# A graph network kernel on one core: row sums of the adjacency by ScalarE instead of TensorE products, adjacency loads behind x, and part of the rows of the first loop by ScalarE

## The chip, the core and the metric

The kernel runs on one core of a Trainium2 chip. A core has five engines with a queue each: TensorE (PE in the profile), VectorE (DVE), ScalarE (ACT), GpSimd (POOL) and SyncE (SP), and 16 DMA engines that all queues share. The metric is the device time of one execution in microseconds, lower is better.

## What is computed

The reference runs four graph layers on x of shape (8, 2048, 64), each followed by a residual and a layer norm. All use one 2048 x 2048 matrix adj of zeros and ones with a diagonal of ones. Only the first two layers matter here:

```python
# layer 0: attention over hyperedges (g), mixed with a mean over neighbours (industry)
deg = jnp.maximum(adj.sum(-1), 1.0)[:, None]
industry = jnp.einsum('nm,bmf->bnf', adj / deg, x @ W_ind)
pair = jnp.stack([industry, g], axis=2)
coefs2 = jax.nn.softmax(attn_scores(pair), axis=-1)
out = jnp.einsum('bnk,bnkf->bnf', coefs2, pair)
# layer 1: symmetric normalisation
A_td = A + jnp.eye(n)
dinv = jax.lax.rsqrt(jnp.sum(A_td, axis=1))
A_hat = dinv[:, None] * A_td * dinv[None, :]
X_p = jnp.einsum('bnd,kd->bnk', jnp.einsum('bmd,nm->bnd', X, A_hat), W)
```

Both need the row sums of adj (the degrees): layer 0 as a reciprocal, layer 1 as an inverse root.

## The kernel before

The eight batches are four pairs p (two batches of 64 features fill 128 partitions). The adjacency is held in SBUF transposed, as 16 row tiles t of 128 rows, each in two halves g of 1024 columns: 32 loads of 512 KB by `load_adj` on POOL's queue (line 214). A product of x with the adjacency is split in a high and a low part so that it keeps its accuracy: for each pair and each half g, 16 tiles x 2 parts x 2 column chunks = 64 passes of 128x512 (line 175, helper `mm`).

The stages that the change touches, in order of time:

1. *The loop over h* (lines 568 to 617). For each of 16 tiles t: products of x with W into `ph` (two buffers in PSUM), clipped scores `seen` (585) and `lr` (592) on VectorE, two small exponentials on ScalarE (590, 596), two VectorE products into the row store `st` (599), one into `ex` (603), and the product `pagg` (609). Each pair of tiles is stored to HBM from ScalarE's queue (607). Five halves of adjacency are issued ahead of the loop behind the loads of x tiles 1 and 3 (`after`, 458), and five more within it, after tiles 1, 3, 5, 7 and 9 (`paced`).
2. *The slot stage* (lines 743 to 780). 16 tiles of rows, gathered in an order by degree, have 12, 5, 5, 4, 4, 4, 3, 3, 3, 3, 2, 2, 2, 2, 2 and 1 slots: 57. A slot is three products into `pz` (three buffers), a VectorE product (765), an exponential `y` on ScalarE (767), two VectorE operations (769, and 774 or 772) and an addition to `acc` on POOL (775). Beside each slot the loop draws five passes from the generator `products` (`fill(5)`, 757) and three more per tile (`fill(3)`), and issues two adjacency loads on POOL until all are out.
3. *The mix stage* (lines 958 to 986): 16 steps (pair p, chunk c) that weigh the neighbour mean against g. Each step loads a chunk of `u0_hbm` and of `inv_hbm` (`mix_load`, 810) and draws four times 8 or 9 passes from `all_pairs`, which gives what is left of `products` and then the products of layer 1 for each pair. Layer 1 of pair p needs the mixed chunks of pair p, stored, loaded again and scaled by `dinv` (`l1_parts`, 888). What is left after the last step is drawn behind it (the tail).

`products` (line 318) gives the 8 x 64 passes of u = adj times x, and behind the first of them 64 passes with a matrix of ones: `degrees` (322) multiplies `ones_r` by every tile, so that the column sums of the transposed adjacency stand in `du`. `inverses` (335) turns them to columns by four transposes, makes `dinv` on POOL (343) and the reciprocal on VectorE (344, 345), and writes the latter spread over 128 partitions to `inv_hbm`.

The order of each engine's queue is fixed when the program is built. TensorE's follows the text (`keep_in_program_order`), POOL's in part, while ScalarE's and VectorE's are set by a scheduler, from buffers and its own times. Each queue is worked in order.

Of the kernel before, what the change touches and what calls it, by code (L numbers as in the profile page):

```python
# [56 lines left out]
def tile_gnn_fast(  # L57
# [3 lines left out]
    x_n: bass.AP,  # L61
    x_t: bass.AP,
    adj_t: bass.AP,
    h_nt: bass.AP,
    h_e2: bass.AP,
    first: bass.AP,
# [31 lines left out]
    def cols(c, n=C):  # L98
        return slice(c * n, (c + 1) * n)
# [74 lines left out]
    def mm(*args, **kw):  # L174
        tc.keep_in_program_order(nc.tensor.matmul(*args, **kw))  # L175
# [40 lines left out]
    def adj_c(t, c):  # L216

        return adj[t][c // 2][:, cols(c % 2)]
# [6 lines left out]
    ones_r = hy.tile([P, P], F32R, name="ones_r")  # L225
    nc.vector.tensor_copy(ones_r, ones)
# [4 lines left out]
    deg4 = hy.tile([P, C], F32, name="deg4")  # L231


    HROW = BF + 8 + E
# [69 lines left out]
            pending.pop(0)[1]()  # L304

    places = {}
    xc, part = {}, {}

    mixed, free = set(), set()
# [8 lines left out]
    def products():  # L318

        deg1 = hy.tile([P, NT], F32, name="deg1")  # L320

        def degrees(g):
            du = pph.tile([P, 2, C], F32, tag="ph", name=f"du{g}", bufs=2)
            for t in range(NT):
                for i in range(2):
                    mm(
                        du[:, i, :], lhsT=ones_r, rhs=adj_c(t, 2 * g + i), start=t == 0, stop=t == NT - 1
                    )
                    yield
            for i in range(2):  # L330
                c = 2 * g + i
                r = slice(c * P // NCH, (c + 1) * P // NCH)
                evacuate(deg4[r, :], du[r, i, :])

        def inverses():

            pdc = places["small"]([P, JT, P], "pdc")
            for j in range(JT):
                transpose(pdc[:, j, :], deg4[:, cols(j, P)])
            pdc = pdc.rearrange("p j (c r) -> p c j r", c=NCH)[:, :, :, 0]  # L340
            d1 = deg1.rearrange("p (c j) -> p c j", c=NCH)
            nc.vector.tensor_scalar(d1, pdc, 1.0, None, op0=ALU.add)
            nc.gpsimd.tensor_tensor(dinv, deg1, neg_half[:, :NT], ALU.pow)
            nc.vector.tensor_scalar(d1, pdc, 1.0, None, op0=ALU.max)
            nc.vector.reciprocal(deg1, deg1)
            for _ in range(8):
                yield
            for c in range(NCH):
                pt = places["small"]([P, C], "pinv")
                for j in range(JT):  # L350
                    k = c * JT + j
                    transpose(pt[:, cols(j, P)], deg1[:, k:k + 1].to_broadcast([P, P]))
                row = va.tile([P, C], F32, tag="ut", name="inv", bufs=2)
                nc.scalar.copy(row, pt)
                nc.sync.dma_start(inv_hbm[:, cols(c)], row)
                for _ in range(4):
                    yield

        for p in range(NP):
            for g in range(2):  # L360
                own = (2 * g, 2 * g + 1)
                ug = pph.tile([P, 2, C], F32, tag="ph", name="ug", bufs=2)
                u = {c: ug[:, c % 2, :] for c in own}
                turning = inverses() if p == 0 and g == 1 else iter(())
                for t in range(NT):
                    for i in range(2):
                        for c in own:
                            mm(
                                u[c], lhsT=part[t // JT][i][:, t % JT, :], rhs=adj_c(t, c),
                                start=t == 0 and i == 0, stop=t == NT - 1 and i == 1,  # L370
                            )
                            tick()
                            if t > 1:
                                next(turning, None)
                            yield
                    if p == NP - 1 and g == 1 and t % JT == JT - 1:
                        first_parts(t // JT, free)
                    if p + 1 < NP and t % JT == JT - 1:
                        c = t // JT
                        if g == 1:  # L380
                            parts(p + 1, c)
                        if g == 1 and c < 2 or g == 0 and c >= 2:
                            fetch(p + 1, (c + 2) % NCH)
                if p == NP - 1:

                    for t in range(g * NT // 2, (g + 1) * NT // 2):
                        onto_diagonal(t, nc.gpsimd, ALU.add)
                for c in own:
                    ut = va.tile([P, C], F32, tag="ut", name="ut", bufs=2)
                    nc.scalar.copy(ut, u[c])  # L390
                    nc.sync.dma_start(u0_hbm[p][:, cols(c)], ut)
                if p == 0 and g == 0:
                    yield from degrees(0)
                    yield from degrees(1)

    def fill(n):
        for _ in range(n):
# [13 lines left out]
    with tc.tile_pool(name="pa_ps", bufs=1, space=PSUM) as pps:  # L411
# [159 lines left out]
        for t in range(NT):  # L571
# [56 lines left out]
        for c in (2, 3):  # L628
            fetch(0, c)
            parts(0, c)  # L630
        for t in range(len(paced) + 5, NT):
            load_adj(t, 0)
        to_load = [(t, 1) for t in range(NT)]
        pa_scope.close()
# [79 lines left out]
    with ExitStack() as pb_scope:  # L714
# [33 lines left out]
        for k, t in enumerate(tiles):  # L748
            S, both, ohs, R, co = now
            acc = pl.tile([P, B, F], F32, tag="acc", name="acc", bufs=2)  # L750
            for s in range(S):
                pz = pps.tile([P, C], F32, tag="mm", name="pz", bufs=3)
                for i, (l, r) in enumerate(((ident_r, both[0]), (ident_r, both[1]), (ohs[s], tab2))):
                    mm(pz, lhsT=l, rhs=r, start=i == 0, stop=i == 2)
                if s == 0 and k + 1 < NT:
                    fill(3)
                    now = begin(tiles[k + 1])
                fill(5)
                for _ in range(2):
# [5 lines left out]
                nc.vector.tensor_tensor(z, z, R[:, s, :, None].to_broadcast([P, B, F]), ALU.mult)  # L765
                y = pl.tile([P, B, F], F32, tag="y", name="y", bufs=3)
                nc.scalar.activation(y, z, AF.Exp, bias=-1.0)
# [42 lines left out]
    def mix_load(i):  # L810
        if i < steps:
            p, c = divmod(i, NCH)
            uts[i] = mp0.tile([P, C], F32, tag="ut0", name="ut0", bufs=2)
            nc.sync.dma_start(uts[i], u0_hbm[p][:, cols(c)])
            invs[i] = mp0.tile([P, C], F32, tag="inv0", name="inv0", bufs=2)
            nc.sync.dma_start(invs[i], inv_hbm[:, cols(c)])

    def mix_ind(i):
# [135 lines left out]
            yield from layer1(p)  # L954


    remaining = filler
    filler = all_pairs()
    mix_load(0)
# [492 lines left out]
def tile_gnn_general(  # L1452
# [640 lines left out]
    "emb", "emb_t", "w_pool", "b_pool", "iv", "w31_t", "b31", "w32_t", "b32",  # L2093
)
FAST = (
    "x_n", "x_t", "adj_t", "h_nt", "h_e2", "first", "mixing", "w1_t", "emb", "emb_4", "w_pool", "b_pool",
    "iv", "w31_t", "b31", "w32_t", "w32", "b32",
)


# [88 lines left out]
```

## Time and profile before

| | |
|---|---|
| device time, median of 3 runs | 1979.12 us (1975.02 to 1979.89) |
| the profiled execution | 1976.23 us, of which the profile's span is 1974.4 us |
| mean granted TensorE clock in it | 0.98 |
| TensorE busy | 1870.6 us (95% of the span) |
| VectorE busy | 1001.6 us (51%) |
| ScalarE busy | 394.6 us (20%) |
| GpSimd busy | 530.7 us (27%) |
| moved by DMA | 143.10 MB, mean 72 GB/s |

The profile is one execution recorded by the hardware; the span is what it covers, a little less than the time of that execution. Busy shares are means over stages with different limits. Matmuls are pipelined, so that their recorded lengths overlap: what a pass costs is read from the distance of two starts. "Idle before" names how long an engine stood still before an instruction and who released it. What an edit is worth is read from the stage that it is in: which wait ends last there.

### The profile page before, as it was taken

What the parts mean: (1) busy time and instruction counts of PE and PEld (TensorE: products, weight loads), DVE (VectorE), ACT (ScalarE), POOL (GpSimd) and SP (SyncE); (2) the same over time, 40 slices, a digit from 0 to 9 for tenths busy, and PEclk for the clock granted to TensorE, in tenths of its full rate; (3) what the DMA queues carried; (4) which work ended last, traced back from release to release, by engine and by line L of the source; (5) the groups of instructions that cost most, each with busy time, mean ns of one, the idle gap of its engine ahead of it and who ended that gap; (6) DMA issues with size and microseconds to landing.
All of it is one profiled execution on the core that took longest, in us unless ns stands there. A gap on an engine that the chain in (4) does not pass through costs nothing.

```text
span 1974.4 us, 19582 instructions
## 1 busy us (share of the span) xinstructions
PE 1870.6 (95%) x7100; PEld 1214.4 (62%) x7100; DVE 1001.6 (51%) x1741; ACT 394.6 (20%) x771; POOL 530.7 (27%) x480
## 2 busy tenths in 40 slices
PE   6888899888799999999999999999999999999997
PEld 4666566555554444755565575556546787877875
DVE  7779555556432211347546736764786333343332
ACT  1455343333121121100000000000001222222211
POOL 3678654544254344301001100110001020100101
PEclk9999899899899999999999999999999999999998
DMA  9923334332400000301101110111101122121211
GB/s 310 314 88 106 125 123 145 125 115 71 155 17 27 0 27 22 119 30 49 64 35 43 55 50 27 48 62 35 43 32 34 38 55 52 46 56 48 54 27 24
DMA packets 94185, 143.10 MB, mean 72 GB/s; under 512 B 29232, under 2 KB 40112, under 8 KB 93696
## 3 DMA queue, kind: packets, MB, share of 16 engines
q1 hardware_dynamic: 83920, 105.39, 17.2%
q0 software_dynamic: 7760, 27.66, 4.2%
q10 hardware_dynamic: 2400, 8.72, 1.2%
q8 instruction: 58, 0.95, 0.2%
q14 instruction: 47, 0.39, 0.1%
HBM read 98.67 MB, written 43.06 MB: 72 GB/s over the span
## 4 chain that ended last, share of the span: by engine, by line
PE 76%; DVE 4%; DMA 4%; POOL 4%; issue 3%; ACT 1%; SPq 1%; POOLq 0%; DVEq 0%; ACTq 0%
PE u L175 32%; PE py L175 22%; PE ua L175 11%; PE ug L175 3%; PE pr L175 2%; POOL ln_r L154 2%; PE po L175 1%; PE pf L175 1%; PE pt L178 1%; PE s L175 1%; DMA x<-x_hbm 1%; POOL r L906 1%; DMA r<-in_x_n 1%; DMA x_hbm<-r 1%; PE pd L175 0%
## 5 line engine op out<-in xcount | busy, mean ns | idle before, releaser
L175 PE MATMUL py<-wp,xg 128*128 128x512 f32 x1024 | 475.2, 592 | 0.7 <-DMA xg<-u_hbm 0.7
L175 PEld LDWEIGHTS py<-wp,xg 128*128 128x128 f32 x1024 | 193.3, 189 | 161.4 <-issue 138.5
L1276 DVE TENSOR_TENSOR fcav<-py,emb_n 128x512 f32<-128x512 f32 x256 | 177.0, 691 | 134.9 <-PE py L175 129.1
L175 PE MATMUL ua<-pt,xn 128*128 128x512 f32 x512 | 230.2, 592 | 1.5 <-DVE pt L1058 1.5
L154 POOL TENSOR_TENSOR ln_r<-ln_e,neg_half 128x8 f32<-128x8 f32 x64 | 108.1, 1688 | 458.0 <-DVE ln_e L152 425.0
L1277 DVE TENSOR_REDUCE r<-fcav 128x32 f32<-128x512 f32 x256 | 175.6, 686 | 8.2
L175 PEld LDWEIGHTS ua<-pt,xn 128*128 128x128 f32 x512 | 96.9, 190 | 110.9 <-issue 104.0
L175 PE MATMUL u<-adj,v0h 128*128 128x512 f32 x384 | 148.7, 455 | 1.3 <-ACT h L1432 1.3
L175 PE MATMUL u<-adj,v0l 128*128 128x512 f32 x384 | 141.3, 436 | 0.0
L175 PE MATMUL u<-adj,v2l 128*128 128x512 f32 x384 | 139.9, 429 | 1.2 <-DVE v2l L171 1.2
L175 PE MATMUL u<-adj,v2h 128*128 128x512 f32 x384 | 141.0, 433 | 0.0
L175 PE MATMUL u<-adj,v1h 128*128 128x512 f32 x384 | 140.7, 433 | 0.0
L175 PE MATMUL u<-adj,v3l 128*128 128x512 f32 x384 | 138.7, 426 | 0.0
L175 PE MATMUL u<-adj,v1l 128*128 128x512 f32 x384 | 138.4, 427 | 0.0
L175 PE MATMUL u<-adj,v3h 128*128 128x512 f32 x384 | 138.3, 427 | 0.0
L1063 POOL TENSOR_TENSOR acc<-acc,pt 128x512 f32<-128x512 f32 x60 | 76.8, 1280 | 103.9 <-DVE pt L1058 103.2
L1058 DVE TENSOR_SCALAR pt<-pt 128x512 f32<-128x512 f32 x64 | 30.2, 472 | 146.5 <-ACT pt L1057 146.2
L1358 DVE SCALAR_TENSOR_TENSOR ar<-fcav,ar 128x512 f32<-128x512 f32 x64 | 45.4, 709 | 109.1 <-ACT ar L1357 109.1
L175 PEld LDWEIGHTS u<-adj,v0h 128*128 128x128 f32 x384 | 71.6, 191 | 37.3 <-issue 24.5
L175 PEld LDWEIGHTS u<-adj,v2l 128*128 128x128 f32 x384 | 72.4, 190 | 32.2 <-issue 16.4
L175 PEld LDWEIGHTS u<-adj,v1l 128*128 128x128 f32 x384 | 72.8, 190 | 29.2 <-issue 14.4
L175 PEld LDWEIGHTS u<-adj,v3l 128*128 128x128 f32 x384 | 72.0, 188 | 29.4 <-issue 14.9
(354 smaller groups left out, 2669.5 us busy)
## 6 DMA issues: line engine op xcount, KB each, us to landing
adj<-in_adj_t POOLq DMA_DIRECT2D x32, 512.0 KB, 7.5
fcav<-in_adj_t SPq DMA_DIRECT2D x64, 256.0 KB, 2.9
u_hbm<-ut SPq DMA_DIRECT2D x48, 256.0 KB, 2.9
xg<-u_hbm SPq DMA_DIRECT2D x96, 128.0 KB, 2.9
x_hbm<-r SPq DMA_DIRECT2D x28, 256.0 KB, 2.1
hs_hbm<-st ACTq DMA_DIRECT2D x8, 584.0 KB
xt<-in_x_t SPq DMA_DIRECT2D x16, 256.0 KB, 6.6
ut<-u_hbm SPq DMA_DIRECT2D x16, 256.0 KB, 3.1
```

Of the source, the lines that this page charges most:

```text
L154: nc.gpsimd.tensor_tensor(rstd, vare, neg_half[:, :groups], ALU.pow)
L175: tc.keep_in_program_order(nc.tensor.matmul(*args, **kw))
L178: tc.keep_in_program_order(nc.tensor.transpose(dst, src, ident))
L906: nc.gpsimd.tensor_tensor(r, r, x1, ALU.add)
L1058: nc.vector.tensor_scalar(pt, pt, 1.0, None, op0=ALU.max)
L1063: nc.gpsimd.tensor_tensor(accs[c], accs[c], pt, ALU.add)
L1276: nc.vector.tensor_tensor(pr, py, e_b, ALU.mult)
L1277: nc.vector.tensor_reduce(r[:, j, b, cols(k, OH)], pr, AX.X, ALU.add)
L1358: nc.vector.scalar_tensor_tensor(ar.bitcast(F32), seen_a, 1.0, ar.bitcast(F32), op0=ALU.mult, op1=ALU.not_equal, accum_out=left[:, t, k:k ...
```

## The change

The degrees no longer come from products. The adjacency is given a second time in its natural layout (`adj_n`), and 32 pieces of 128 rows by 1024 columns are loaded on SP's queue into two buffers; ScalarE sums each along its row (`accum_out`). The generator `inverses` with these sums starts at pass 90 of the products instead of behind them. The reciprocals get a buffer of their own (`degs`). The two buffers of the pieces are later those of the mix stage's chunks. In the loop over h, adjacency loads wait for the first eight x tiles; two instead of five are issued ahead of the loop, seven within it, seven behind it. Of the two products into `st` one stays on VectorE and the other becomes four activations. In the slot stage's first tile four passes are drawn beside each slot instead of five.

```diff
-    def degrees(g):
-            du = pph.tile([P, 2, C], F32, tag="ph", name=f"du{g}", bufs=2)
-            for t in range(NT):
-                for i in range(2):
-                    mm(
-                        du[:, i, :], lhsT=ones_r, rhs=adj_c(t, 2 * g + i), start=t == 0, stop=t == NT - 1
-                    )
...
+        def inverses():
+            halves = [(t, g) for t in range(NT) for g in range(2)]
+            loaded = []
+            def load():
+                if halves:
+                    t, g = halves.pop(0)
+                    piece = mp0.tile([P, 2, C], F32, tag="uti", name="piece", bufs=2)
+                    flat = piece.rearrange("p k c -> p (k c)")
+                    nc.sync.dma_start(flat, adj_n[t * P:(t + 1) * P, g * N // 2:(g + 1) * N // 2])
+                    loaded.append((flat, t, g))
+            load()
+            load()
+            while loaded:
+                for _ in range(6):
                     yield
+                flat, t, g = loaded.pop(0)
+                nc.scalar.activation(flat, flat, AF.Identity, accum_out=deg2[:, t, g:g + 1])
+                load()
+            nc.vector.tensor_tensor(degs, deg2[:, :, 0], deg2[:, :, 1], ALU.add)
+            nc.vector.tensor_scalar(deg1, degs, 1.0, None, op0=ALU.add)
             nc.gpsimd.tensor_tensor(dinv, deg1, neg_half[:, :NT], ALU.pow)
-            nc.vector.tensor_scalar(d1, pdc, 1.0, None, op0=ALU.max)
-            nc.vector.reciprocal(deg1, deg1)
+            nc.vector.tensor_scalar(degs, degs, 1.0, None, op0=ALU.max)
+            nc.vector.reciprocal(degs, degs)
...
-                            if t > 1:
-                                next(turning, None)
+                            passes += 1
+                            if passes == 90:
+                                turning.append(inverses())
+                            if turning:
+                                next(turning[0], None)
                             yield
...
-                if p == 0 and g == 0:
-                    yield from degrees(0)
-                    yield from degrees(1)
...
-        for t in range(5):
-            if t in (0, 2):
-                after(xt[1 + t][:, 0, 0:1])
+        after(xt[2 * XB - 1][:, 0, 0:1])
+        for t in range(2):
             load_adj(t, 0)
...
-        paced = {1: 5, 3: 6, 5: 7, 7: 8, 9: 9}
+        paced = {1: 2, 3: 3, 5: 4, 7: 5, 9: 6, 11: 7, 13: 8}
...
-            for k in range(2):
-                nc.vector.scalar_tensor_tensor(
-                    st[:, k * G * F:(k + 1) * G * F].rearrange("p (g f) -> p g f", f=F), hv[:, k, :, 0:F], 1.0,
-                    e_gn[:, k * G:(k + 1) * G, None].to_broadcast([P, G, F]), op0=ALU.add, op1=ALU.mult,
+            nc.vector.scalar_tensor_tensor(
+                st[:, 0:G * F].rearrange("p (g f) -> p g f", f=F), hv[:, 0, :, 0:F], 1.0,
+                e_gn[:, 0:G, None].to_broadcast([P, G, F]), op0=ALU.add, op1=ALU.mult,
+            )
+            for g in range(G):
+                b = G + g
+                nc.scalar.activation(
+                    st[:, b * F:(b + 1) * F], hv[:, 1, g, 0:F], AF.Identity, bias=e_gn[:, b:b + 1], scale=e_gn[:, b:b + 1]
                 )
...
-                fill(5)
+                fill(4 if k < 1 else 5)
...
-            uts[i] = mp0.tile([P, C], F32, tag="ut0", name="ut0", bufs=2)
+            both = mp0.tile([P, 2, C], F32, tag="uti", name="uti", bufs=2)
+            uts[i], invs[i] = both[:, 0, :], both[:, 1, :]
...
+    for _ in turning[0]:
+        pass
     remaining = filler
```

More of the change, by code (lines that the diff above doesn't have):

```diff
@@ L63, in tile_gnn_fast @@
     adj_t: bass.AP,
+    adj_n: bass.AP,
     h_nt: bass.AP,
@@ L223, in onto_diagonal @@
         eng.tensor_tensor(block, block.bitcast(F32), ident, op)
-    ones_r = hy.tile([P, P], F32R, name="ones_r")
-    nc.vector.tensor_copy(ones_r, ones)
     number = hy.tile([P, 12], F32, name="number")
@@ L229, in tile_gnn_fast @@
         nc.gpsimd.memset(number[:, i:i + 1], -1.0 - i)
-    deg4 = hy.tile([P, C], F32, name="deg4")
+    deg2 = hy.tile([P, NT, 2], F32, name="deg2")
     HROW = BF + 8 + E
@@ L306, in tile_gnn_fast @@
     places = {}
+    turning = []
     xc, part = {}, {}
@@ L320, in products @@
         deg1 = hy.tile([P, NT], F32, name="deg1")
-        def degrees(g):
-            du = pph.tile([P, 2, C], F32, tag="ph", name=f"du{g}", bufs=2)
-            for t in range(NT):
-                for i in range(2):
-                    mm(
-                        du[:, i, :], lhsT=ones_r, rhs=adj_c(t, 2 * g + i), start=t == 0, stop=t == NT - 1
-                    )
-                    yield
[L330 to L342, printed above, removed]
+        degs = hy.tile([P, NT], F32, name="degs")
+        def inverses():
[12 more added lines that the diff above has]
+                for _ in range(6):
+                    yield
+                flat, t, g = loaded.pop(0)
[3 more added lines that the diff above has]
+            nc.vector.tensor_scalar(deg1, degs, 1.0, None, op0=ALU.add)
             nc.gpsimd.tensor_tensor(dinv, deg1, neg_half[:, :NT], ALU.pow)
-            nc.vector.tensor_scalar(d1, pdc, 1.0, None, op0=ALU.max)
-            nc.vector.reciprocal(deg1, deg1)
+            nc.vector.tensor_scalar(degs, degs, 1.0, None, op0=ALU.max)
+            nc.vector.reciprocal(degs, degs)
             for _ in range(8):
@@ L351, in inverses @@
                     k = c * JT + j
-                    transpose(pt[:, cols(j, P)], deg1[:, k:k + 1].to_broadcast([P, P]))
+                    transpose(pt[:, cols(j, P)], degs[:, k:k + 1].to_broadcast([P, P]))
                 row = va.tile([P, C], F32, tag="ut", name="inv", bufs=2)
@@ L357, in inverses @@
                     yield
+        passes = 0
         for p in range(NP):
@@ L363, in products @@
                 u = {c: ug[:, c % 2, :] for c in own}
-                turning = inverses() if p == 0 and g == 1 else iter(())
                 for t in range(NT):
@@ L630, in tile_gnn_fast @@
             parts(0, c)
-        for t in range(len(paced) + 5, NT):
+        for t in range(len(paced) + 2, NT):
             load_adj(t, 0)
@@ L812, in mix_load @@
             p, c = divmod(i, NCH)
-            uts[i] = mp0.tile([P, C], F32, tag="ut0", name="ut0", bufs=2)
+            both = mp0.tile([P, 2, C], F32, tag="uti", name="uti", bufs=2)
+            uts[i], invs[i] = both[:, 0, :], both[:, 1, :]
             nc.sync.dma_start(uts[i], u0_hbm[p][:, cols(c)])
-            invs[i] = mp0.tile([P, C], F32, tag="inv0", name="inv0", bufs=2)
             nc.sync.dma_start(invs[i], inv_hbm[:, cols(c)])
@@ L2095 @@
 FAST = (
-    "x_n", "x_t", "adj_t", "h_nt", "h_e2", "first", "mixing", "w1_t", "emb", "emb_4", "w_pool", "b_pool",
-    "iv", "w31_t", "b31", "w32_t", "w32", "b32",
+    "x_n", "x_t", "adj_t", "adj_n", "h_nt", "h_e2", "first", "mixing", "w1_t", "emb", "emb_4", "w_pool",
+    "b_pool", "iv", "w31_t", "b31", "w32_t", "w32", "b32",
 )
@@ L2146 @@
         "x_t": xt,
+        "adj_n": a["adj"],
         "x_n": xn,
```

## The prediction

> **What bounds the kernel now.** I read the page's slices first, then busy time by stretches, then the DMA queues, the waits and the timeline of each stage that the change touches. Four slices of the page:
>
> ```profile
> PE   6888899888799999999999999999999999999997
> ACT  1455343333121121100000000000001222222211
> DMA  9923334332400000301101110111101122121211
> GB/s 310 314 88 106 125 123 145 125 115 71 155 17 27 0 27 22 119 30 49 64 35 43 55 50 27 48 62 35 43 32 34 38 55 52 46 56 48 54 27 24
> ```
>
> A slice is 49 us. From about 550 us on TensorE is 9 tenths busy in almost every slice and the change touches nothing there. It touches the first eleven slices: the loop over h (to 54 us), the slot stage (65 to 235), the mix stage (239 to 493) and its tail (to 556). In the first two slices the DMA engines are full. Stretches:
>
> ```profile
> 60.00:80.00 20.00, 18.56 (x80) 14.93 (x79) 14.33 (x39) 8.49 (x27) 15.56 (x21) 0.83 1.01 343
> 80.00:100.00 20.00, 16.73 (x69) 11.82 (x69) 14.26 (x23) 8.60 (x23) 15.34 (x19) 1.00 1.10 364
> 100.00:120.00 20.00, 17.98 (x79) 13.64 (x78) 19.74 (x34) 11.31 (x31) 14.99 (x12) 1.00 0.15 53
> ...
> 160.00:180.00 20.00, 18.52 (x87) 14.67 (x86) 19.62 (x32) 10.13 (x29) 17.26 (x14) 1.00 0.25 81
> ```
>
> The columns are PE, PE load, DVE, ACT, POOL, granted clock, DMA share, GB/s. To 100 us the transfers are saturated (share 1.0 to 1.1); from 100 us VectorE is (19.6 to 19.7 of 20), and TensorE has slack. A product that leaves this stage therefore buys little in it. What fills the DMA engines is this, from the DMA view of 70 to 80 us:
>
> ```profile
> q0 software_dynamic: 1118, 4.10, 112.9%
> issues: line engine op xcount, KB each, median us to landing
> adj<-in_adj_t POOLq DMA_DIRECT2D x7, 512.0 KB, 7.5
> ```
>
> 4.10 MB in 10 us is 410 GB/s, all of it adjacency, and a half row block takes 7.5 us to land. In the slot stage's first tile ScalarE's timeline shows how the exponentials (y) hang on VectorE:
>
> ```profile
> 75.71 0.60 ACT L767 ACTIVATE y<-pz 128x512 f32<-128x512 f32 x1 [1.36 <-DVE pz L765]
> 77.68 0.60 ACT L767 ACTIVATE y<-pz 128x512 f32<-128x512 f32 x1 [1.36 <-DVE pz L765]
> 79.70 0.60 ACT L767 ACTIVATE y<-pz 128x512 f32<-128x512 f32 x1 [1.42 <-DVE pz L765]
> ```
>
> One slot each 1.97 us, ScalarE idle two thirds of it: room in time, but the queue is in order. Mix stage and tail, by stretches, and the largest wait of TensorE in 340 to 550 us:
>
> ```profile
> 240.00:302.00 62.00, 62.00 (x260) 38.39 (x259) 31.47 (x44) 25.91 (x44) 31.62 (x28) 0.97 0.46 149
> 302.00:493.00 191.00, 165.08 (x708) 107.45 (x706) 108.68 (x160) 65.03 (x111) 95.26 (x72) 0.95 0.34 110
> 493.00:556.00 63.00, 50.08 (x225) 40.00 (x226) 29.67 (x57) 11.14 (x21) 19.46 (x13) 0.87 0.39 132
> ```
>
> ```profile
> PE po L175 <- ACT ut L948: 20.5, 4, 8.6
> ```
>
> TensorE is gapless while the filler is products, has 26 us of gaps once layer 1 mixes in, and 13 in the tail.
>
> **What the Trainium skill says.** "ScalarE: Activation LUTs", section What ACT_TABLE_LOAD costs: 186 ns plus 0.833 ns per element, 93 ns more for each per-partition scale or bias, and neighbours overlap by about 93 ns. The trace agrees: 0.21 us for 8 elements, 0.60 for 512, 0.39 for 128 with a bias. "DMA: Bandwidth & Descriptors", section Issuing engines are not separate DMA queues: transfers from SP, ACT and GpSimd share the same 16 engines and interleave, so another queue adds no bandwidth; its section Queues, rings and completion order says that each engine takes turns between queues, a packet at a time. The trace bears this out where it can: with adjacency in flight a 256 KB xc load on SP's queue took 5.7 us, against 2.1 for a 256 KB store when the engines were free.
>
> **The change, part by part** (against the profiled execution: 1976.2 us, span 1974.4; the median of the runs is 1979.1, so 2.9 above it).
>
> *Products for degrees.* 2 x 16 x 2 = 64 passes of 128x512 leave. Passes start 0.233 us apart (five du passes from 104.70, next group at 105.86), so 14.9 us of TensorE, with four transposes (0.5). The fills take their passes by count: 20 before the slots, 15 x 3 + 57 x 5 in them, in all 350 of 576 + 512. After: 338 (one less in each of tile 0's 12 slots). So tile 0 sheds 12 passes (2.8 us), and the mix stage begins with 174 products left instead of 226. It uses 588 passes either way; the tail then has 98 instead of 150. The whole rest of the gain, 52 x 0.233 = 12.1 us, falls in the tail, and only if the mix does not stall more.
>
> *Mix and tail.* Layer 1 comes 52 passes earlier, some 1.5 of the 16 steps. The steps from 318 to 493 us took 17.3 us each (175 us over 10.1 steps) against 14 for their work (36 x 0.233; 5.1 of mix products, since a step with 32 passes and no layer 1 took 12.53 in the chain of waits; 0.5 for layer 1's own small products), so 1.5 steps more with layer 1 cost 5 us. Part (2,3) now has about 18 passes between storing and use, and (3,3) 20, where there were 70; its chain of store 2.1, load 2.7, scaling 1.3, split 1.3 is longer than the latter: 2 us. Sum -5, between -12 (nothing stalls) and +4 (both parts stall 8 us).
>
> *Degrees by ScalarE.* 32 sums of 128x1024: 186 + 853 = 1.04 us, 33 us of ScalarE, not seen in the trace (nearest row 0.60 for 512). 32 loads of 512 KB on SP, 16.8 MB. The generator asks for the first at pass 90, in tile 1's fourth slot, but the built order puts them far ahead: on ScalarE two sums stand before y of tile 0's second slot, 7 before its fifth, 16 before its eleventh. Every y behind a sum waits for that sum's load, and VectorE, the three slot buffers and then TensorE wait for y; POOL's adjacency issues stand between its acc additions, so they wait too. That is in the saturated stretch. Before, 62 to 98 us moved 13.8 MB. After, it must also carry 16 pieces (8.4 MB) and one more adjacency tile (0.5): 22.7 MB at 0.405 MB/us is 56 us instead of 36, so +20 if all must land. Some adjacency is not needed until later, so I take +16. Bounds: -2 (pieces slip through, 12 passes saved) and +24 (pieces, with two buffers against five or six adjacency tiles in flight, get the small share). The other 16 sums fall in tiles 1 to 5, where ScalarE's 11 of 20 us rises to 16 or more but a slot takes about 2.7 us: +4. There VectorE loses a stall,
>
> ```profile
> DVE deg L344 <- POOL dinv L343: 4.7, 1, 4.7
> ```
>
> since dinv and the maximum no longer share a buffer, and two 0.69 copies: -6. Together -2, between -6 and +8. SP's u0 stores and xc loads stand behind 14 and more piece loads; their consumers come tens of us later, so nothing.
>
> *Half the rows by ScalarE.* In the loop VectorE works 24.1 of 29 us (25 to 54 us), 1.78 a tile; one product (0.38 of it) goes. ScalarE gets four activations with two pointer operands: 186 + 186 + 53 = 425 ns, 332 apart: with 0.43 for the two exponentials and 0.17 for store issues about 1.8 us a tile. The bound changes engine and hardly moves: 0, from -4 to +3. *Adjacency behind x* removes no wait that the trace shows (none of TensorE's waits there names xt) and moves one tile behind the loop: 0, within the last bounds.
>
> Sum: -5 + 16 - 2 + 0 = +9 us; 1976 + 9 = 1985, on the median 1988.
>
> **Rivals.** *The sums fit in.* If the queues share so that a piece lands every 2.6 us and y is early enough, tile 0 costs -2, later tiles -6, mix and tail -9: -17, 1962. For it: ScalarE's idle two thirds. Against: 400 GB/s already used. It decides when sums delay tile 0 by less than 7 us; then the kernel is not slower. *A draw:* tile 0 at +7: 1979. *ScalarE becomes the bound:* +24 in tile 0, +8 in later tiles, +3 in the loop, -4 in the mix: +31, 2010. For it: tile 1 needs 8 us of ScalarE's old work and 5.2 of sums for five slots. *The change does not do what it says*, that is, sums start at the pass it names: then the adjacency has landed, and the fitting-in case results; the built order speaks against it.
>
> **Numbers.** Forecast 0.42 (1982 to 1999), fits in 0.30, draw 0.13, ScalarE bound 0.15. A measurement of this kernel tells 0.3%, 6 us. Slower by more: 0.42 + 0.15, less 0.02 at the forecast's lower edge, 0.55; within 0.15; faster 0.30. The range 1961 to 2008 leaves out some of the first and last rival, 0.1 each.
>
> **What would show it.** Right: in tile 0, y or the sum waiting for the piece's DMA, the slots some 3.5 us apart, DMA share 1.0 until about 115 us, TensorE's slot stage ending some 14 us late, and a tail shorter by 8 to 12. Wrong: sums with no DMA wait, or the loop over h ending before 50 us. The forecast falls if tile 0 ends within 42 us of the first adjacency issue after the loop (36 now).

## The result, and the profile after

The changed kernel takes 2035.5 us (median of 4 runs, 2028.3 to 2036.4) against 1978.3 before (4 runs, 1975.0 to 1979.9): a ratio of 1.0283, 95% interval 1.0256 to 1.0311. It is slower, as forecast, but by 57 us and not by 9. Its profiled execution has a span of 2034.6 us against 1974.4, so 60 us are to be found.

The stages are marked off by TensorE's instructions, whose first and last starts the view of a tile gives (pz: the slots' products; pt: the transposes that end each mix step; the third layer's scores; pr: the last layer's products):

| us | before | after | difference | forecast |
|---|---|---|---|---|
| start to first pz (the loop over h ends at 54.1 and 70.5) | 65.1 | 82.7 | +17.6 | 0 |
| first to last pz: slot stage | 157.5 | 188.9 | +31.4 | +14 |
| last pz to first score: mix and tail | 334.0 | 343.3 | +9.3 | -5 |
| of these, first to last pt | 237.3 | 263.9 | +26.6 | |
| of these, last pt to first score: tail | 62.7 | 46.0 | -16.7 | -12 |
| first score to last pr | 1369.9 | 1371.6 | +1.7 | 0 |

Nearly all of it lies in the first 615 us. The slices of the page after, for PE, DMA and GB/s (one slice is 51 us):

```profile
PE   5758889886779999999999999999999999999997
DMA  7786343333240000031111121111010222121211
GB/s 255 246 302 216 112 152 130 115 113 95 81 145 13 26 26 16 10 126 36 44 53 34 49 63 34 42 55 48 31 43 27 48 51 52 39 61 47 52 31 23
```

The transfers now last through three slices, and in the third TensorE is at 5 tenths, where before it had 8. The same stretches as before (PE, PE load, DVE, ACT, POOL, granted clock, DMA share, GB/s), of the kernel after:

```profile
60.00:80.00 20.00, 16.82 (x67) 11.41 (x67) 10.80 (x24) 8.68 (x27) 6.70 (x9) 0.68 0.41 130
80.00:100.00 20.00, 14.87 (x58) 11.42 (x57) 12.35 (x33) 10.23 (x28) 10.33 (x15) 0.83 1.06 377
100.00:120.00 20.00, 8.59 (x22) 5.97 (x22) 6.93 (x11) 7.59 (x13) 7.56 (x10) 0.67 1.04 373
160.00:180.00 20.00, 15.20 (x60) 11.55 (x60) 19.32 (x26) 15.95 (x41) 17.46 (x15) 0.88 0.67 209
```

From 100 to 120 us no engine works more than 43% of the time, and the transfers are full. From 160 us on VectorE is at its limit again (19.3 of 20 us). The timeline of ScalarE, with VectorE and TensorE behind it, shows who waits for what:

```profile
105.55 1.06 ACT L342 ACTIVATE piece<-piece 128x1024 f32<-128x1024 f32 x1 [4.17 <-DMA piece<-in_adj_n]
106.51 0.19 ACT L342 ACTIVATION_READ_ACCUMULATOR piece<-piece 128x1 f32 x1
...
108.17 1.06 ACT L342 ACTIVATE piece<-piece 128x1024 f32<-128x1024 f32 x1 [1.47 <-DMA piece<-in_adj_n]
...
113.38 1.06 ACT L342 ACTIVATE piece<-piece 128x1024 f32<-128x1024 f32 x1 [4.06 <-DMA piece<-in_adj_n]
...
114.43 0.58 ACT L773 ACTIVATE y<-pz 128x512 f32<-128x512 f32 x1
115.04 0.69 DVE L775 SCALAR_TENSOR_TENSOR y<-pz,y 128x512 f32<-128x512 f32 x1 [10.18 <-ACT y L773]
115.88 0.77 PE L176 MATMUL pz<-hrh,ident_r 128*128 128x512 f32 x1 [10.83 <-DVE y L775]
```

Four sums stand between two exponentials y here; the last three are shown. Each of the three waits 1.5 to 4.2 us for its piece; when y has run, VectorE has waited 10.2 us for it, and TensorE 10.8 us for a slot buffer. The exponentials of tile 0, first to last, took 31.1 us before and take 60.1 now.

In the loop over h, by the waits of 12 to 65 us, VectorE waits for TensorE (6.3 us before) and TensorE for VectorE (7.2 before):

```profile
DVE seen L587 <- PE ph L576: 21.0, 13, 2.9
PE pagg L615 <- DVE ex L609: 16.3, 11, 2.9
```

None of the engines is at its limit: from 25 to 54 us VectorE is busy 12.8 of 29 us (24.1 before), ScalarE 18.0, TensorE 17.3. Something makes them take turns. In the mix and its tail, from 275 to 615 us, TensorE's longest wait is one that did not occur before:

```profile
PE u L176 <- ACT v3h L171: 21.3, 3, 16.2
```

### The profile page after: what moved, and what is told of

Same layout as the page of the kernel before. It is cut to its first block, busy times and chain, and to the rows that moved or that the text cites. A ratio compares the mean times of both kernels' runs of the same rounds, so it can differ in the third digit from the quotient of the medians.

```text
span 2034.6 us, 19592 instructions
## 1 busy us (share of the span) xinstructions
PE 1880.8 (92%) x7032; PEld 1218.4 (60%) x7032; DVE 1009.9 (50%) x1723; ACT 447.0 (22%) x897; POOL 528.5 (26%) x481
## 4 chain that ended last, share of the span: by engine, by line
PE 72%; DMA 4%; DVE 4%; POOL 3%; issue 2%; ACT 1%; SPq 1%; POOLq 0%; ACTq 0%; DVEq 0%
PE u L176 31%; PE py L176 22%; PE ua L176 11%; PE pr L176 2%; POOL ln_r L155 2%; PE ug L176 1%; DMA y<-x_hbm 1%; PE po L176 1%; DMA x_hbm<-r 1%; DVE r L158 1%; PE s L176 1%; PE pt L179 1%; PE pf L176 1%; POOL y L901 1%; DVE ln_v L151 0%
## 5 line engine op out<-in xcount | busy, mean ns | idle before, releaser
L176 PEld LDWEIGHTS u<-adj,v3h 128*128 128x128 f32 x384 | 72.0, 189 | 51.8 <-ACT v3h L171 22.6
L176 PEld LDWEIGHTS u<-adj,v2h 128*128 128x128 f32 x384 | 72.1, 192 | 35.4 <-issue 15.6
```

## The experiments

All stage lengths are of one profiled execution of each kernel; times are medians of 2 to 10 runs, with the ratio to the kernel before, run on the same chip. "Mix" stands for mix and tail together (last pz to first score). In the runs that leave the text of the loop over h as changed, its last pagg starts anywhere from 66.1 to 75.5 us (70.5 in the changed kernel), so differences of a few us in that stage are not read as effects.

| run | time | ratio (95%) | first pz | slots | mix |
|---|---|---|---|---|---|
| rows_dve | 2021.6 | 1.0210 (1.0192 to 1.0228) | 66.4 | 187.1 | 343.5 |
| rows_pinned | 2034.2 | 1.0269 (1.0250 to 1.0287) | 80.2 | 190.5 | 344.6 |
| ex_first | 2027.9 | 1.0241 (1.0214 to 1.0267) | 74.6 | 189.4 | 343.6 |
| split_ph | 2021.7 | 1.0208 (1.0191 to 1.0226) | 72.0 | 187.7 | 342.6 |
| deg_products | 1995.0 | 1.0067 (1.0043 to 1.0090) | 83.3 | 157.6 | 333.9 |
| pin_sums | 2022.4 | 1.0209 (1.0182 to 1.0235) | 87.7 | 172.3 | 343.2 |
| no_sums | 2034.9 | 1.0278 (1.0248 to 1.0308) | 82.9 | 187.0 | 345.3 |
| no_loads | 2011.2 | 1.0159 (1.0130 to 1.0187) | 82.3 | 166.6 | 342.8 |
| pin_noloads | 2002.9 | 1.0131 (1.0107 to 1.0156) | 77.2 | 159.3 | 341.9 |
| mix_k8 | 2025.7 | 1.0239 (1.0214 to 1.0264) | 83.6 | 189.0 | 325.2 |
| mix_k8_before | 1956.1 | 0.9894 (0.9876 to 0.9913) | 65.3 | 157.5 | 310.2 |
| fill4 | 2017.0 | 1.0196 (1.0179 to 1.0213) | 84.0 | 192.8 | 317.3 |
| fill6_before | 1997.8 | 1.0112 (1.0095 to 1.0129) | 66.7 | 163.2 | 344.9 |
| fill4_k8 | 2017.8 | 1.0206 (1.0189 to 1.0223) | 82.5 | 189.8 | 319.6 |
| repaired | 1997.1 | 1.0104 (1.0087 to 1.0121) | 67.8 | 174.9 | 325.2 |
| repaired_spaced | 1987.7 | 1.0054 (1.0037 to 1.0071) | 66.7 | 168.5 | 325.0 |
| best | 1984.3 | 1.0029 (1.0020 to 1.0039) | 67.6 | 171.9 | 323.0 |
| split_k8 | 1959.2 | 0.9900 (0.9883 to 0.9916) | 69.3 | 162.0 | 308.3 |

### Which part costs what: rows_dve and deg_products

The first undoes the half of the rows by ScalarE; the second keeps it and the order of the loads, and undoes all that concerns the degrees.

```diff
# rows_dve: the changed kernel with
+            for k in range(2):
+                nc.vector.scalar_tensor_tensor(st[:, k * G * F:(k + 1) * G * F]..., hv[:, k, :, 0:F], 1.0, ...)
-            for g in range(G):
-                nc.scalar.activation(st[:, b * F:(b + 1) * F], hv[:, 1, g, 0:F], AF.Identity, ...)
```

> The changed kernel with both row products of the loop over h on VectorE again; adjacency behind x and the sums by ScalarE stay. Changed kernel: last product of the loop (pagg) at 70.5 us against 54.1 before, first pz at 82.7 against 65.1. Theory A (the half by ScalarE costs the loop 16 us): last pagg at 53 to 57 us, time 2016 to 2022. Rival B (the adjacency behind x makes the loop late): last pagg stays near 70 us, time 2035. If A holds but the slot stage then meets the adjacency loads earlier and fuller, the loop ends early and the time still falls by less than 10 us.

> The degrees by TensorE products as before (with five passes beside each slot of tile 0), the loop over h and the adjacency order as changed. Theory: the slot stage is 158 us again, and mix and tail (from the last pz to the start of the third layer's scores, 334 us before and 343 after) are 334 us again, so that only the loop's 17 us remain: 1993 to 1998. Rival: the 9 us more in mix and tail come from the late start or the loop and stay: 2002 to 2007.

Both came as the theory had it. With the rows on VectorE the loop ends at 54.9 us, so ScalarE's half costs 16 us of loop, and the adjacency behind x about 1. With the degrees by products the slot stage is 157.6 and the mix 333.9, though the adjacency still comes behind x: both growths belong to the degrees, and only the late start remains (first pz at 83.3). The loss in the loop is separate from the other two.

### Why the loop is slow: rows_pinned, ex_first, split_ph

In the changed kernel VectorE took the clip (seen) of the next tile ahead of this tile's product into ex, which it mostly had not done before. The clip waits for TensorE's ph of that next tile, and ex starts right behind the clip. Was it that order?

```diff
# rows_pinned: VectorE's seen and ex each in
+            tc.keep_in_program_order(nc.vector....)
```

> The changed kernel, ScalarE's half kept, but VectorE's order held as the text has it: the product into ex of tile t ahead of the clip (seen) of tile t+1, as it mostly stood before. Theory C (the loop is slow because VectorE's new order puts ex behind the next tile's clip, so that TensorE's ph, VectorE's seen and ex and TensorE's pagg follow one another, 2.72 us a tile): pitch falls to 1.9 to 2.2 us a tile, last pagg at 56 to 61 us, time 2020 to 2026. Rival D (ScalarE's four activations, which hold a buffer of ph until they are done, are the bound whatever the order): pitch stays at 2.6 to 2.8, last pagg near 70, time 2033 to 2037.

It was not that order alone: the pitch, the time from one tile to the next, is 2.9 us instead of 2.7 (1.9 before), and the last pagg starts at 67.8. The timeline of this run shows another wait that is at least as long (from the start of one tile's activations):

```profile
32.41 1.29 ACT L606 ACTIVATE st<-ph,st 128x64 f32<-128x64 f32 x4 [0.28 <-DVE st L600]
33.73 0.69 DVE L609 TENSOR_TENSOR ex<-ph,ex 128x512 f32<-128x512 f32 x1 [1.42 <-ACT st L606]
34.34 0.17 DVE L587 TENSOR_SCALAR seen<-ph 128x16 f32<-128x16 f32 x1
...
34.54 0.21 ACT L592 ACTIVATE st<-seen 128x8 f32<-128x8 f32 x1 [0.84 <-DVE seen L587]
...
34.78 0.42 DVE L600 SCALAR_TENSOR_TENSOR st<-ph,st 128x256 f32<-128x256 f32 x1
...
35.30 1.29 ACT L606 ACTIVATE st<-ph,st 128x64 f32<-128x64 f32 x4 [0.28 <-DVE st L600]
```

The product into ex needs nothing that the activations make, yet it starts when the last of them has ended (32.41 + 1.29), some 0.03 us behind it in each of the 16 tiles. In the changed kernel too it starts 0.03 to 0.35 us behind it in 15 of 16 tiles, so there both waits end nearly together. Both instructions read ph. The Trainium skill, page "PSUM — Partial Sum Buffer", section PSUM bank collisions raise a hardware error, says that two engines must not be in the same PSUM bank at once on the same partitions, reads against reads included, and that a compiler keeps them apart with a dependency. The trace agrees: in rows_pinned no read of one ph by ScalarE lies beside one by VectorE. Two runs test it, one with another order of the readers, one with a buffer for each half and another order as well.

```diff
# ex_first
+            nc.vector.tensor_tensor(ex[:, :, :, 0:F], hv[:, :, :, 0:F], ...)
             for g in range(G):
                 nc.scalar.activation(st[:, b * F:(b + 1) * F], hv[:, 1, g, 0:F], ...)
-            nc.vector.tensor_tensor(ex[:, :, :, 0:F], hv[:, :, :, 0:F], ...)
# split_ph
-            ph = pph.tile([P, 2, C], F32, tag="ph", name="ph", bufs=2)
+            ph = [pph.tile([P, C], F32, tag=f"ph{k}", name=f"ph{k}", bufs=2) for k in range(2)]
```

> The changed kernel with the product into ex (VectorE) written ahead of ScalarE's four activations instead of behind them; nothing is left out. In the run with VectorE's order held, each ex product began when the last of the four activations of the same tile ended (waits of 1.4 us, 21.6 in all), so a tile was the sum of clip, exponential, VectorE's product, 1.29 of activations and 0.69 of ex: 2.9 us. Theory J (the readers of one ph follow one another in the text's order, whichever engine they are on): with ex ahead, no ex waits for them, the activations lie beside the next tile, pitch 1.8 to 2.3 us, last pagg at 54 to 61, time 2019 to 2027. Rival D (ScalarE's 1.29 us a tile in which ph is held is the bound): pitch 2.6 or more, last pagg 67 or more, time 2033 or more.

> The changed kernel with each half of ph (four batches[...]) in a buffer of its own, and the products in the order: ex of the second half (VectorE), then the second half of the rows (ScalarE), beside it the first half of the rows and ex of the first half (VectorE); clip and ex become two instructions each. Theory J (readers of the same PSUM buffer follow one another, so that ScalarE's 1.29 us stood in the middle of VectorE's work): VectorE now works on one half while ScalarE has the other, its own work is some 1.75 us a tile, pitch 1.8 to 2.1, last pagg at 53 to 58 us against 70.5, time 2018 to 2026. Rival D (ScalarE's four activations a tile are too slow for the loop, shared buffer or not): pitch 2.3 or more, last pagg 62 or more.

With ex first the wait turns round (the activations now wait for ex), pairs of tiles take 5.16 us, and the last pagg is at 61.1: 9 of 16 us regained by order alone. With separate buffers pairs take 4.98 us and the last pagg is at 59.6: 11 of 16. There VectorE does work beside the activations, on the other half:

```profile
31.28 0.75 DVE L610 TENSOR_TENSOR ex<-ph,ex 128x256 f32<-128x256 f32 x2
31.79 1.29 ACT L617 ACTIVATE st<-ph,st 128x64 f32<-128x64 f32 x4 [0.78 <-DVE ex L610]
```

Neither run reached the pitch that theory J gave: 2.58 and 2.49 us came, and the second lies in its rival's range. So it is shown that more than half of the loss hangs on where the activations stand among the reads of ph. That the shared buffer as such makes it is not shown: splitting it, with a new order, gave 1.5 us more than order alone, which is less than this stage varies. Some 5 us stay. ScalarE is not busy all the time either (18.2 of 29 us): in split_ph its half still waits for ex of its half, and the exponential of the next tile stands behind it. What share each has was not taken apart.

### What the sums cost in the slot stage: pin_sums, no_sums, no_loads, pin_noloads

```diff
# pin_sums: sums and exponentials y in the order of the text
-                nc.scalar.activation(flat, flat, AF.Identity, accum_out=deg2[:, t, g:g + 1])
+                tc.keep_in_program_order(nc.scalar.activation(flat, flat, AF.Identity, accum_out=...))
-                nc.scalar.activation(y, z, AF.Exp, bias=-1.0)
+                tc.keep_in_program_order(nc.scalar.activation(y, z, AF.Exp, bias=-1.0))
# no_sums, with deg2 set to a constant
-                nc.scalar.activation(flat, flat, AF.Identity, accum_out=deg2[:, t, g:g + 1])
# no_loads: nc.sync.dma_start(flat, adj_n...) for t == 0 alone
# pin_noloads: pin_sums and no_loads together
```

> The changed kernel with the order of sums and exponentials y on ScalarE held as the text has it: the first sum stands behind y of tile 1's fourth slot or so, one sum for each slot from there. Theory E (in tile 0 each y stands behind sums that wait for their piece, which took tile 0 from 33 to about 64 us): tile 0 back to 33 to 38 us, a sum's wait for its piece under 5 us in all, time 2003 to 2012. Rival F (ScalarE has too much to do with 32 sums of 1.25 us in the slot stage, wherever they stand): the stage stays at 180 us or more, time 2025 to 2036.

> The changed kernel with the 32 loads of pieces but without the 32 sums (left out: the degrees, which stand as a constant). The loads are then bound to nothing but each other and come one behind the other at full rate. Theory E (exponentials y queued behind sums that wait for their piece make tile 0 long): tile 0's y from first to last within 31 to 45 us (31.1 before, 60.1 after), slot stage 158 to 172 us of pz (157.5 before, 188.9 after), time 2004 to 2020. Rival I (the 16.8 MB themselves delay adjacency and rows, whoever waits for a sum): slot stage stays at 183 or more, time 2030 or more.

> The changed kernel with all 32 sums but with two loads of pieces alone: the same two pieces are summed again and again (left out: the other 30 loads, so the degrees are not those of the matrix). The sums stand as far ahead of the exponentials y as in the changed kernel. Theory E: no sum but the first two waits, tile 0 takes 31 to 40 us, slot stage 158 to 168, time 2004 to 2016. Rival F (ScalarE's 32 x 1.25 us of work in a queue in order cost it, without any wait for data): slot stage 175 or more, time 2020 or more. What is above 157.5 here is the price of the work, the rest of the 31.4 that of the waits.

> The changed kernel with the order of sums and y held as the text has it and with two loads of pieces alone (left out: the other 30, so the degrees are not those of the matrix). Slot stage 172.3 with all loads, 166.6 with two loads and the order not held. If waits for pieces make what is left above 157.5: 158 to 163 us. If the work of 32 sums does: 166 or more, as much as without the order held.

With the order held tile 0 takes 32.7 us (31.1 before), but the slot stage is still 172.3: the sums wait elsewhere (16.8 us for pieces), and the time came out 10 us above what was expected, some 5 of them because the loop ended later. With two loads alone, the sums still far ahead, the stage is 166.6 (and tile 0 42.3 us, where at most 40 were expected); with both edits 159.3. So of 31.4 us the loads make 22.3, the place of the sums without them 7.3 more, and ScalarE's 32 x 1.25 us of work in good order 1.8. Taken in the other order the place makes 16.6 and the loads 13.0: most of the loss needs both.

The run without sums missed its number: 187.0. Yet tile 0 is short in it (36.2 us), and one wait holds the rest, by the waits of 130 to 172 us:

```profile
ACT v2h L171 <- DMA xc<-in_x_n: 29.2, 1, 29.2
DVE y L775 <- ACT y L773: 28.8, 2, 28.6
```

A 256 KB load of xc, issued on SP, stands behind the pieces in SP's queue until 162.9 us, and ScalarE's queue behind that. 187.0 less 28.6 is 158.4, an estimate, since no run takes away this wait alone. By it the 16.8 MB themselves cost the slots little. Adjacency took 13.7 us to land instead of 7.5, and all transfers together moved 395 GB/s from 80 to 130 us, where before adjacency alone had 410 from 70 to 80. This agrees with the Trainium skill's page "DMA: Bandwidth & Descriptors", section Issuing engines are not separate DMA queues, that another queue adds no bandwidth. What costs here is who is queued behind a transfer that is late.

### Why the mix is longer with less work: mix_k8, mix_k8_before, fill4, fill6_before, fill4_k8

The wait of 16.2 us for v3h, in the timeline of the kernel after (SP's store of the mixed chunk and load of it, POOL's scaling, ScalarE's split, TensorE's product):

```profile
508.30 0.32 SPq L885 DMA_DIRECT2D x_hbm<-r  x1
510.93 0.32 SPq L900 DMA_DIRECT2D y<-x_hbm  x1
514.01 1.04 POOL L901 TENSOR_TENSOR y<-y,dinv 128x512 f32<-128x512 f32 x1 [6.46 <-DMA y<-x_hbm]
515.09 0.62 ACT L171 CAST v3h<-y 128x512 fp32r<-128x512 f32 x1 [11.31 <-POOL y L901]
515.75 1.22 PE L176 MATMUL u<-adj,v3h 128*128 128x512 f32 x2 [16.20 <-ACT v3h L171]
```

TensorE was ready for v3h at 499.6 us, 8.7 us before the store of the chunk was even issued.

```diff
# mix_k8 (on the changed kernel), mix_k8_before (on the kernel before)
-        k = 9 if i > NCH else 8
+        k = 8
```

> The changed kernel, but the mix stage draws 8 passes at each of its four places in every step instead of 9 from the sixth step on (45 passes fewer, which go to the tail; nothing is left out). Theory G (52 products fewer are left when the mix begins, so that layer 1 comes up to the mixed chunk before it is stored, loaded and split, and TensorE stands behind v3h for 16 us): that wait falls under 5 us, mix (pt first to last) 263.9 to 226 to 242, tail 46 to 55 to 63, from last pz to the third layer's scores 343 to 322 to 331, time 2013 to 2025. Rival H (the mix is slow for what the change adds elsewhere, such as the two loads into one buffer pair or the later dinv): sum stays above 338, time 2031 to 2037.

> The kernel before the change with 8 passes at every place of the mix. Theory G says that the kernel before had products enough (no wait for v3h in its mix), so that 45 passes only move to the tail: sum from last pz to the third layer's scores 334 within 6, time 1974 to 1986. Rival: the mix gains from fewer passes whatever was left, and the gain in the changed kernel says nothing of the products that it lacks: sum 322 or less, time 1970 or less.

The edit took 18 us off the changed kernel's mix, and its wait for v3h went (the time fell by 10 us only, as the stage behind became 5 us longer). But it took 24 us off the mix of the kernel before, which had no such wait: it gains whatever was left, as the rival had it, so the first run proves nothing about the missing products. (In the kernel before, TensorE's waits for ut fell from 20.5 to 1.9 us.) The next runs change the number of products left and nothing in the mix itself: 219 instead of 174 in the changed kernel, 169 instead of 226 in the kernel before.

```diff
# fill4, with the sums drawn every 5 passes from pass 87, so that they stand at the same slots
-                fill(4 if k < 1 else 5)
+                fill(4)
# fill4_k8: this and the edit of mix_k8
# fill6_before
-                fill(5)
+                fill(6)
```

> The changed kernel, but with four passes beside each slot in all tiles, so that 219 products are left when the mix begins (174 in the changed kernel, 226 before); the sums are drawn every 5 passes from pass 87, so that they stand at the same slots. Theory G (the mix is longer because it begins 52 products shorter and so mixes more of its steps with layer 1): mix back from 263.9 to 235 to 242 us, no wait for v3h over 5 us, sum from last pz to the third layer's scores 343 to 328 to 336, slot stage as it was (186 to 192), time 2022 to 2029. Rival K (the mix is longer for something else in the change, as its shared buffers or the later dinv): sum stays at 340 to 346, or grows, time 2033 or more.

> The mirror of it: the kernel before the change with six passes beside each slot, so that 169 products are left when the mix begins instead of 226; nothing is left out. Theory G: this kernel now shows what the changed one did: a wait for v3h of 10 us or more, mix 237 to 255 to 270, tail 63 to 44 to 52, sum 334 to 340 to 348, slot stage 157 to 162, time 1984 to 1996. Rival K: mix and tail as before, only 13 us moved between them, sum 320 to 336, time 1966 to 1981.

> Both: four passes beside each slot and 8 at every place of the mix. With 8 everywhere the kernel before had 310 us from last pz to the third layer's scores, the changed one 325 with 52 products fewer left. Theory G: 304 to 314 here, time 1998 to 2010. Rival K: 320 or more, time 2016 or more.

The mix follows the number left, in both kernels and both ways: 317.3 instead of 343.3, and 344.9 instead of 334.0; fill4 shows no wait for v3h. The kernel before, short of products, shows the changed one's mark among TensorE's waits:

```profile
PE u L175 <- ACT v3h L170: 20.6, 4, 13.9
```

So products that are missing bring this wait and the longer mix about. The number left is not all, though: with 219 the changed kernel's mix is 17 us under that of the kernel before with 226, and under the 328 to 336 expected; why stays open. With 8 passes as well the mix was 319.6, not the 304 to 314 expected: in the tail TensorE stands 13.9 us before one product (pb). The trace names no engine for it, but shows that ScalarE's operation on the same data (el), just ahead of pb, waits for the load of the embeddings, which SP issues at 535.6 us, when TensorE has stood since 531.1.

### All together: repaired, repaired_spaced, best, split_k8

The first joins rows_dve, pin_sums and mix_k8; the second draws the sums from pass 60 every 8 passes; best adds fill4 to the first, with sums from pass 55 every 6; split_k8 is the kernel before with the rows split as in split_ph and 8 passes in the mix.

> The changed kernel with three of the parts above put together: both row products on VectorE, the order of sums and exponentials y held as the text has it, 8 passes at every place of the mix. If the three causes are separate, their gains add up: 13.9 (rows on VectorE) + 13.1 (order held) + 9.8 (mix) off 2035.5, so 1999 (1993 to 2005). If they lie on one another (for example the order held is worth less where the slot stage starts earlier and meets the adjacency loads), 2006 to 2016.

> As the run before it, but the sums begin at pass 60 and are 8 passes apart instead of 6, so that a load has more of the time of two slots to land before its sum, and the sums reach nearly to the end of the slot stage. If the waits for pieces make the rest of the loss (16.8 us of them in the run with the order held): slot stage 158 to 166 us instead of 172, time 8 to 14 us under the run before it. If ScalarE's work among the exponentials makes it: slot stage 169 or more, same time within 5 us.

> All repairs at once: rows of the loop on VectorE, order of sums and y held, sums from pass 55 every 6 passes, four passes beside each slot, 8 at every place of the mix. Sum of parts: loop as before (pz from 66), slot stage 165 to 174, then 305 to 314, and 1372 to 1378 to the end: 1960 to 1980 against 1956 for the kernel before with 8 passes. If it is above 1956, nothing of the 15 us of removed products is left after all repairs; if under 1950, the idea pays once its order is right.

> The kernel before the change with three things: half the rows by ScalarE in the form of the run before this one (each half of ph in its own buffer), 8 passes at every place of the mix, and nothing else (degrees by products, adjacency as before). The kernel before with 8 passes alone took 1956. If the half by ScalarE is worth anything once it no longer stands in VectorE's way, 1950 to 1955; if VectorE's two more instructions a tile eat it, 1955 to 1961; slower than 1961 if the loop still waits for ScalarE.

The gains add up (1997.1 against 1999). An earlier start of the sums and wider spacing give 9 us more, of which 6.4 in the slot stage (168.5, between the two ranges expected). But best, for which the sum of the parts had given 1960 to 1980, stays 6.6 us above the kernel before, and by the ratios some 27 above the kernel before with 8 passes, which with 1956.1 us is the fastest of all and has nothing of the change in it. Against that one its slot stage is 14 us longer and its mix 13; 8 of the 13 are the wait at pb (14.3 us against 6.6). Nor does the half by ScalarE add anything to the kernel before with 8 passes (1959.2).

## Why the prediction was right or wrong

The direction was right for the reason named, the sums in tile 0. That loss was forecast too small, and those of the loop and the mix, 27 of the 60 us, were not foreseen.

**Products removed, mix and tail: -5 forecast, +9.3 measured.** The counts were right: the mix begins 52 products short, the tail sheds them (-16.7 us against -12), and layer 1 begins 1.5 steps sooner. The step that failed is "Part (2,3) now has about 18 passes between storing and use". There was no such slack (18 x 0.233 = 4.2 us): TensorE came to that part 8.7 us before its store was issued, and waited 16.2 us. The 5 us for more steps with layer 1 were too few as well: steps 5 to 15 took 19.4 us each instead of 16.9. fill4 and fill6_before show that this hangs on the number left.

**Degrees by ScalarE: +16 in tile 0 and -2 later forecast; 29 and 3 measured** (exponentials first to last 31.1 to 60.1; from the next one to the last 123.9 to 127.3). The mechanism was the one named: y behind sums, sums behind pieces, and the transfers full until some 130 us. The bytes were right too: from the first adjacency load behind the loop (77.8 us) until tile 0's 16th piece had landed (142.6 us) 22.5 MB moved, and the forecast had 22.7. The step that failed is "Some adjacency is not needed until later, so I take +16". The pieces, two in flight, came in pairs some 8 us apart (97.5, 105.6, 113.4 us) and had 4.2 of the 11.0 MB moved from 100 to 130 us. So it was they that landed last, and tile 0 had to wait for nearly everything. This took 64.8 us, at 347 GB/s, and not 56 us at 405; less the 36 us of before it is 29, as much as tile 0 lost (a sum, not an experiment). The upper bound of +24 had named this case and was still too low. Bytes alone do not do it: no_sums moved 22.8 MB from 78 to 139 us and left tile 0 at 36.2 us. A sum's own price was nearly right, 1.06 us (forecast 1.04); not counted were 0.19 us more for a separate instruction that reads the accumulator.

**"SP's u0 stores and xc loads stand behind 14 and more piece loads; their consumers come tens of us later, so nothing"**: this held in the changed kernel, where waits pace the loads; in no_sums it cost 28.6 us.

**Half the rows by ScalarE: 0 (-4 to +3) forecast, +16 measured.** The step was "about 1.8 us a tile. The bound changes engine and hardly moves". It took the pitch for the larger of two engines' sums, as if they worked side by side. They took turns at ph: ex came behind the 1.29 us of activations in its tile, and pagg, the next products into ph and the next clip came behind ex. The pitch was 2.72 us. ScalarE's own price was about right (1.29 us for four, worked out 1.42). How much the order of the readers and how much the shared buffer makes stays open; order alone gave back 9 of 16 us.

**Adjacency behind x: 0 forecast, about 1 measured** (last pagg at 54.9 us in rows_dve against 54.1). Right.

**The rivals.** "ScalarE becomes the bound" (2010) was nearest, yet in no stretch shown here is ScalarE busy throughout: it waits. The two runs in which all sums but the first two find their data bring the slot stage to 159 to 167 us, which leaves "the sums fit in" its point: the work does fit.

## What to carry to other kernels

Work moved to an idle engine is paid for by its place in that engine's queue: ask what each moved instruction waits for, and who stands behind it, and price a wait by the load that lands last: here the pieces, with two buffers, got 4.2 of 11.0 MB while the transfers were full. Two engines that read the same PSUM buffer took turns here instead of sharing its work. Before work is split between engines, look at the order of the reads and at the buffer; here even both together did not make the split pay. Products that serve as filler hide latencies in a later stage; before removing some, look at which wait they cover there, and measure the number left as a setting of its own.

## What the runs showed that was not expected

A sum on ScalarE with an accumulator is two instructions, 1.06 and 0.19 us for 1024 columns. Four activations of 64 columns with two pointer operands took 1.29 us: each 0.41 us long, with 0.29 us from one start to the next, less than the 332 ns worked out. And the granted clock from 100 to 120 us was 0.67 with TensorE busy 43% of the time, where before it was 1.00 with 90%; from 120 to 130 us before it was 1.00 with 59%. What sets it these runs don't tell.
